# Weights in three loads, one batch's last sums on ScalarE, and a shared last step, in a four-block transformer on one core

## The chip, the cores and the metric

The kernel runs on one core of a Trainium2 chip. A core has five engines that run side by side, each through its own list of instructions in order: TensorE (PE) multiplies matrices and transposes through its array, with weight loads (PEld) that overlap its matmuls; VectorE (DVE), ScalarE (ACT) and GpSimd (POOL) work element by element; SyncE (SP) issues DMAs. An engine waits for another only where an instruction of its list waits on a semaphore. The metric is the device time of one execution in microseconds; the time of a kernel is the median of several executions.

## What is computed

Four blocks, each followed by a sum with its input and a layer norm. Everything is float32, with 8 batches of 512 tokens and 256 channels.

```python
x = L0_attn_x                                        # (8, 512, 256)
x = layernorm(x + retention(x, past_kv, W_qkv, ...)) # 16 heads of 16, decay mask
x = layernorm(x + ffn(x, ternary(W_fc), ternary(W_proj)))   # 1024 wide, gelu, inner norm
x = layernorm(x + linear_attention(x, Wq, Wk, Wv, W1, W2))  # over heads in a token
x = layernorm(x + experts(x, w_router, wi, wo))      # 8 experts, top 2, capacity 160
```

The first block takes q, k and v of a batch from `x @ W_qkv`, forms scores with a decay mask in chunks of 128 tokens, and norms the result over the whole batch. The last block chooses two experts for a token, gathers at most 160 tokens per expert in each of two groups (batches 0 to 3 and 4 to 7), runs `relu(x @ wi) @ wo`, and adds the weighted rows to the tokens. The last line is that sum followed by a layer norm, whose result is the output:

```python
m = mean(x, -1); v = var(x, -1)
return (x - m) / sqrt(v + 1e-5)
```

## The kernel before

The whole kernel is one function, `tile_layers`, that lays the order of the instructions of all engines by hand. Each piece of work is a generator ("stage"): `stage_a0` makes q, k, v of half a batch, `stage_a1` the scores and the first attention of a batch, `stage_a2` its norm, `stage_b` the ffn, `stage_bn` its norm, `stage_c1`, `stage_hd`, `stage_ca` and `stage_c2` the third block, `choose` and `route` the routing, and then the gathers, dispatches and experts of each group, and `finish` the last norm of a batch. `finish_last` does the last rows.

A planner in the kernel runs at build time. `op` (L235) books a stretch on an engine from a time and a cost that are written in the stage, and `flush` emits all booked instructions in the order of their planned starts. This is why most instructions have line L235. `pe(cost)` adds a stage's matmuls to PE's planned time. `either` books the engine that would end first, by the costs given. Booking DVE work as `DVS`, or POOL work as `POOL`, also books a resource named "port", so that in the plan the two do not overlap there. `bank` takes one of the eight PSUM banks, `slot_tile` one of a few buffers of a kind, and `give` and `release` hand them back with a time.

`interleave` decides which stage goes on next on PE: it walks the long string `turns`, one letter for each step of a stream of stages, and takes the first stage of it that can go on. Where PE would wait more than 1.4 us in the plan, it puts in filler matmuls, named `spare` (L405). So a changed cost or a changed string moves instructions on all engines.

The places that the change touches:

- The loads at the start. All plain DMAs go through SP's one list, in order: the identity (L99), x of the first half batch by `fetch_half(0)`, all of W_qkv as one load, the other constants `cst`, `past`, and then, from `prepare_ffn`, four loads of W_fc, four of W_proj, and small ones. The second half batch's x follows when `load_x` asks for it.
- `stage_a0`: four transposes of x into PSUM, a copy to `xT` on ACT or DVE, 4 matmuls for q and 4 for k (L1081), then 4 for v (L1107); a float32 matmul takes two passes through the array, and the profile counts passes, so 16 and 8. q is copied by ACT, scaled by the decay table on POOL (`qd`) and masked on ACT (`qz`, L235); k is scaled on DVE (`kT`); v is copied by ACT (`vz`). The scores (`sc`, L1154) need qz and kT.
- `prepare_ffn` sums |W_fc| and |W_proj| on DVE (`fc_t`, `pr_t`), makes them ternary on DVE and transposes them on PE (`fc_tp`, `pr_tp`).
- The exchange of heads in the third block: `stage_c1` writes q and k to DRAM (`q_d`, `k_d`) and v (`v_d`, eight small stores), `stage_hd` reads them back in another order (`hh`, `vt`), and `stage_ca` multiplies them (`hs`, L1608).
- The combination: `combine` transposes an expert's result (`eo_tp`, L1942), scales it on ACT or DVE (`eo`), and POOL adds its rows to `y_d` in DRAM by an indirect DMA. Each of these waits until the one before it has landed.
- `finish(b)` loads `z`, 512 tokens of `y_d`, by SP and calls `layernorm`. For each of four chunks of 128 tokens, DVE makes the statistics (two instructions, L476 and L477), then a small step with epsilon on DVE, the power -1/2 on POOL, a small step for the offset `nb` on DVE, and four normalisations. For the second group these go to ACT or DVE, whichever would end first (`free`). Batches 6 and 7 wait in the plan until the tokens of the last expert are known.
- The last expert's rows do not go through `y_d`. Its results `eo_0`, `eo_1`, `eo_2` are added to the tokens concerned by matmuls with a 0/1 matrix (`tail_ps`, L2025), after the tokens' other sums were fetched (`tail_y`). `finish_last` adds these, makes statistics and normalises on DVE, and POOL writes the rows over the output by indirect DMAs (L2053), which wait for the plain stores of the output.

## Time and profile before

| | us |
|---|---|
| median of 3 runs | 875.41 (874.04 to 876.87) |
| the profiled run | 876.97 |
| span of its profile, first to last instruction | 874.9 |

| engine | busy us | share |
|---|---|---|
| PE | 822.5 | 94% |
| PEld | 674.0 | 77% |
| DVE | 616.0 | 70% |
| ACT | 513.3 | 59% |
| POOL | 323.4 | 37% |

PE's 822.5 us hold 34.7 us of fillers. The mean granted clock of PE is 0.983 of full speed. In the timeline a line has the start, the duration, the engine, the line of the kernel, the operation, out<-in, the shape and the count; in brackets stand the idle time just before it on its engine and what ended that. In the table by stretches, each engine has its busy time and number of instructions, then follow the granted clock, the mean busy share of the DMA engines, and what they moved. Matmul ends are modelled, so "busy" is not "at peak". A wait for several things is put down to the one that came last.

### The profile page before, as it was taken

To read this page: it belongs to the slowest core of one execution; us is meant where nothing else is said; L and a number is where in the kernel's file an instruction comes from. 1 tells how busy PE (TensorE), PEld (TensorE's weight loads), DVE (VectorE), ACT (ScalarE), POOL (GpSimd) and SP (SyncE) were. 2 spreads that over 40 slices of the span, in tenths; PEclk is the share of its full clock that TensorE was granted. 3 is DMA by queue.
4 is the path that set the end of the run, shared out by engine and by line. 5 is a ranking of instruction groups with operands and counts; after the bars stand their busy time and mean duration, and the time that the engine had idled before them with its cause. 6 is when DMAs were issued, how large, how long until landed. Compare 5 with 4: busy or idle time off the path is not lost. (4 is left out here: it accounts for less than half of the span.)

```text
span 874.9 us, 20462 instructions
## 1 busy us (share of the span) xinstructions
PE 822.5 (94%) x8078; PEld 674.0 (77%) x8078; DVE 616.0 (70%) x1677; ACT 513.3 (59%) x1039; POOL 323.4 (37%) x343
## 2 busy tenths in 40 slices
PE   7999989999999999999899999899999999989982
PEld 5877877876878887787778777677679889779971
DVE  4945687588788788877888898899878444604325
ACT  2435668658764867758788686876745364122221
POOL 1222452344244532343254425415153241362432
PEclk9999999999999999999999999999999999999995
DMA  6153111652722032633523528636577477658352
GB/s 209 31 171 114 44 38 18 116 147 54 180 65 60 23 78 54 165 93 37 151 30 79 161 43 227 200 50 174 147 181 241 139 227 243 179 138 268 78 144 91
DMA packets 201647, 106.89 MB, mean 122 GB/s; under 512 B 124464, under 2 KB 192240, under 8 KB 201360
## 3 DMA queue, kind: packets, MB, share of 16 engines
q1 hardware_dynamic: 197696, 100.01, 42.0%
q0 software_dynamic: 3856, 5.57, 3.5%
q8 instruction: 64, 1.05, 0.5%
q14 instruction: 31, 0.25, 0.1%
HBM read 70.96 MB, written 30.41 MB: 116 GB/s over the span
## 5 line engine op out<-in xcount | busy, mean ns | idle before, releaser
L235 POOL TENSOR_TENSOR fsq<-fsq,fh 128x256 f32<-128x256 f32 x96 | 70.3, 732 | 66.2 <-ACT fh L235 42.5
L235 DVE TENSOR_TENSOR scm<-sc,cst 128x512 f32<-128x512 f32 x109 | 68.7, 681 | 13.0 <-PE sc L1154 12.8
L1384 PE MATMUL fc_ps<-x1T,fcT 128*128 128x256 f32 x512 | 72.1, 291 | 4.4 <-DVE x1T L235 4.4
L235 DVE TENSOR_TENSOR hm<-hs,cst 128x512 f32<-128x512 f32 x111 | 70.4, 681 | 8.2 <-PE hs L1608 8.1
L1384 PEld LDWEIGHTS fc_ps<-x1T,fcT 128*128 128x128 f32 x512 | 64.1, 191 | 8.8 <-DVE x1T L235 4.5
L1425 PE MATMUL pr_ps<-prT,fT 128*128 128x258 f32 x512 | 69.3, 290 | 0.0
L235 DVE SCALAR_TENSOR_TENSOR fT<-fh,lnf,fT 128x256 fp32r<-128x256 f32 x128 | 61.1, 524 | 11.3 <-ACT fT L235 10.8
L1425 PEld LDWEIGHTS pr_ps<-prT,fT 128*128 128x128 f32 x512 | 63.8, 189 | 3.1 <-issue 1.6
L1081 PE MATMUL qk_ps<-xT,wqkv 128*128 128x256 f32 x256 | 62.4, 396 | 3.2 <-DMA wqkv<-in_L_attn_W_qkv 1.9
L235 POOL DMA_INDIRECT y_d<-eo,srci x21 | 32.7, 1557 | 82.7 <-issue 22.9
L1900 PE MATMUL wo_ps<-e_hT,wo 128*128 128x160 f32 x416 | 63.2, 305 | 0.0
L1516 PE MATMUL qk_ps<-x2T,l1T 128*128 128x512 f32 x128 | 59.6, 600 | 1.0 <-ACT x2T L235 1.0
L1900 PEld LDWEIGHTS wo_ps<-e_hT,wo 128*128 128x128 f32 x416 | 58.9, 193 | 1.6 <-issue 0.9
L1872 PE MATMUL wi_ps<-xsT,wi 128*128 128x160 f32 x416 | 60.0, 300 | 0.0
L1081 PEld LDWEIGHTS qk_ps<-xT,wqkv 128*128 128x128 f32 x256 | 49.2, 198 | 13.0 <-issue 3.3
L235 ACT ACTIVATE fT<-fh,lnf 128x256 fp32r<-128x256 f32 x128 | 58.2, 499 | 1.5
L1872 PEld LDWEIGHTS wi_ps<-xsT,wi 128*128 128x128 f32 x416 | 57.4, 190 | 0.8 <-ACT xsT L235 0.5
L235 POOL TENSOR_TENSOR ln<-ln,mhalf 128x4 f32<-128x4 f32 x32 | 33.7, 1054 | 56.1 <-DVE ln L235 54.1
L235 ACT ACTIVATE e_hT<-wi_ps 128x480 f32<-128x480 f32 (+1 forms) x48 | 24.8, 523 | 47.0 <-PE wi_ps L1872 45.3
L235 POOL TENSOR_TENSOR scm<-scm,cst 128x512 f32<-128x512 f32 x19 | 24.3, 1281 | 59.8 <-ACT scm L235 22.4
L235 ACT ACTIVATE fh<-fh 128x512 f32<-128x512 f32 x64 | 39.5, 626 | 9.4 <-DVE fT L235 8.4
L1608 PE MATMUL hs<-hh 16*128 16x128 f32 x1024 | 41.1, 292 | 4.1 <-DMA hh<-q_d 2.7
(286 smaller groups left out, 1945.0 us busy)
## 6 DMA issues: line engine op xcount, KB each, us to landing
wi<-in_L_ffn_wi SPq DMA_DIRECT2D x10, 1024.0 KB
wo<-in_L_ffn_wo SPq DMA_DIRECT2D x10, 1024.0 KB
hh<-k_d SPq DMA_DIRECT2D x32, 256.0 KB
hh<-q_d SPq DMA_DIRECT2D x32, 256.0 KB
xh<-in_L_attn_x SPq DMA_DIRECT2D x16, 256.0 KB
x<-in_L_attn_x SPq DMA_DIRECT2D x8, 512.0 KB
k_d<-qk SPq DMA_DIRECT2D x32, 128.0 KB
q_d<-qk SPq DMA_DIRECT2D x16, 256.0 KB
```

Of the source, the lines that this page charges most:

```text
L235: heapq.heappush(Plan.events, (t, Plan.count, shares, t + cost, lambda: fn(*args, **kw)))
L1081: T.matmul(ps[:, m * HT : (m + 1) * HT], wqkv[:, k, which * D + m * P : which * D + (m + 1) * P], xT[:, k, :], start=(k == 0), stop=(k == ...
L1384: T.matmul(ps[:, j * HT : (j + 1) * HT], fcT[:, k, f * P : (f + 1) * P], x[:, k, :], start=(k == 0 and x is low), stop=(k == NK - 1 and x ...
L1425: T.matmul(acc[:, : D + 2], hs[:, part, f, c * P : (c + 1) * P], prT[:, f, :], start=(f == 0 and part == 1), stop=(f == NF - 1 and part == 0),
L1516: T.matmul(ps, l1T[:, k, which, m * P : (m + 1) * P], x2T[:, k, :], start=(k == 0), stop=(k == NK - 1),)
L1608: T.matmul(sc[r][:, g * P : (g + 1) * P], hh[rows, a * D + z : (a + 1) * D : 2], qh[rows, :, 16 * a + z : 16 * a + 16 : 2], start=True, st ...
L1872: T.matmul(ps[:, f * CAP : (f + 1) * CAP], wi[k][:, (f3 + f) * P : (f3 + f + 1) * P], x[:, k, es], start=(k == 0), stop=(k == NK - 1),)
L1900: T.matmul(ps[:, m * CAP : (m + 1) * CAP], parts[2 + f // 4][:, f % 4, m * P : (m + 1) * P], hT[:, f, :], start=(f == 0), stop=(f == NF - 1),)
```

## The change

- W_qkv is loaded in three parts (q, k and v columns), and x of the second half batch right behind them, ahead of the constants.
- `layernorm` gets a form `summed`, used for batch 5: ACT makes the sums of each chunk (a copy with an accumulated output, L235), DVE the mean and its negative (`centres`), ACT the sums of squares about the mean, DVE the variance.
- The second choice for the normalisations of batches 4 to 7 is POOL at 0.56 instead of DVE at 0.42.
- Some 20 planned costs are set to other values, among them the landing of a scatter into `y_d` (2.5 to 3.0) and the start of the last stores.
- The string `turns` is another one.

```diff
-    def layernorm(pool, dst, src, ts, on_act=False, keep=False, free=False):
+    def layernorm(pool, dst, src, ts, on_act=False, keep=False, free=False, summed=False):
...
+        def centres():
+            nc.vector.tensor_scalar(nb, sums[:, 0, :], -1.0 / D, None, ALU.mult)
+            return nc.vector.tensor_scalar(mv[:, :, 0], sums[:, 0, :], 1.0 / D, None, ALU.mult)
...
-        for c in range(NC):
+        if summed:
+            waste = slot_tile(pool, "ex", [P, D], "waste")
+            sums = ln[:, : 2 * NC].rearrange("p (i c) -> p i c", i=2)
+            for c in range(NC):
+                t = op(
+                    ACT, 0.43, max(ts[c], Plan.slot_of[id(ln)][3]), A.activation, waste, src[:, c, :], AF.Copy,
+                    accum_out=sums[:, 0, c : c + 1], use=waste,
+                )
+            t = op(DVS, 0.14, t, centres, use=ln)
+            for c in range(NC):
+                t = op(
+                    ACT, 0.43, t, A.activation, waste, src[:, c, :], AF.Square,
+                    bias=nb[:, c : c + 1], accum_out=sums[:, 1, c : c + 1], use=waste,
+                )
+            give(waste, t)
+            t = op(DVS, 0.08, t, V.tensor_scalar, mv[:, :, 1], sums[:, 1, :], 1.0 / D, None, ALU.mult)
+        for c in range(0 if summed else NC):
             t = op(DVE, 0.61, ts[c], stats, c, use=ln)
...
-                        DVS, 0.42, V.tensor_scalar,
+                        POOL, 0.56, GP.tensor_scalar,
...
-        dma(0.0, wqkv, ins["L0_attn_W_qkv"].rearrange("(k p) n -> p k n", p=P))
+        w_in = ins["L0_attn_W_qkv"].rearrange("(k p) n -> p k n", p=P)
+        for cols in (slice(D), slice(D, 2 * D), slice(2 * D, 3 * D)):
+            dma(0.0, wqkv[:, :, cols], w_in[:, :, cols])
+        fetch_half(1)
...
-            t = Plan.t + (4.0 if i == 0 else 22.0 if i < 4 else 5.0)
-            if i > 0:
+            t = Plan.t + (4.0 if i == 0 else 8.0 if i == 1 else 14.0 if i < 4 else 5.0)
+            if i > 1:
...
-            t = pe(0.36)
+            t = pe(0.3)
...
-                Plan.landed = done + 2.5
+                Plan.landed = done + 3.0
...
-                t = op(POOLD, 1.2, max(t, tail["stored"]), put, j, n)
+                t = op(POOLD, 1.28, max(t, tail["stored"] + 1.2), put, j, n)
...
-            e = max(layernorm(wk, z, z, [landing] * NC, on_act=(g == 1), free=(g == 1)))
+            e = max(layernorm(wk, z, z, [landing] * NC, on_act=(g == 1), free=(g == 1), summed=(b == B - 3)))
...
-            "cbhnbbnbbcblbbnlellnlbeeerblnbeeeeeeleebelllbbbleebcllclllbcleebbbelbeeneblllenrnnnl"
...
+            "nbblbhbcbnbblebllleeccbbnelebeeeeeleeeblnllbbbleelblclllnbcleebbbeelbeenllelnbnnnlnc"
...
```

The order of the built program of each kernel can be listed. In the new one, batch 5's eight sums stand on ACT between the second group's first normalisations and the scaling of `eo_0`; `eo_1` stands behind batch 5's two normalisations on ACT; and two of the four normalisations of each of the batches 4 to 7 stand on POOL. PE has 4845 matmuls instead of 4846, of which 70 instead of 71 are fillers, and three of them stand in the tail.

More of the change, by code (lines that the diff above doesn't have):

```diff
@@ L1161, in scores @@
                         T.transpose(ps[:, m * P : (m + 1) * P], kT[:, m, cs], ident)
-                t = pe(1.35 if c < NC - 1 else 1.0)
+                t = pe(1.32 if c < NC - 1 else 1.04)
                 give(qz[c], t)
@@ L1226, in stage_a1 @@
                             )
-                t = pe(1.95 if c < NC - 1 else 1.55)
+                t = pe(1.97 if c < NC - 1 else 1.58)
                 for sm in scm:
@@ L1293, in stage_a2 @@
             t = op(
-                DVE, 0.15, pe(0.2), V.tensor_scalar, gs[:, 0:1], ps[:, 0:1], -1.0 / P, None, ALU.mult,
+                DVE, 0.15, pe(0.15), V.tensor_scalar, gs[:, 0:1], ps[:, 0:1], -1.0 / P, None, ALU.mult,
                 bank=ps,
@@ L1300, in stage_a2 @@
             T.matmul(ps[:, 0:1], ones, gs[:, 1:2], start=True, stop=True)
-            t = rsqrt(gs[:, 2:3], ps[:, 0:1], 1.0 / P, LN_EPS, pe(0.2), bank=ps)
+            t = rsqrt(gs[:, 2:3], ps[:, 0:1], 1.0 / P, LN_EPS, pe(0.15), bank=ps)
             ga = wk.tile([P, 2, 2], F32, tag="gn_a", name=f"gn_a_{b}")
@@ L1315, in stage_a2 @@
                 e1 = op(
-                    ACT, 0.47, t, A.activation, r[:, 0, :], r[:, 0, :], AF.Identity,
+                    ACT, 0.59, t, A.activation, r[:, 0, :], r[:, 0, :], AF.Identity,
                     bias=ga[:, 1, 0:1], scale=ga[:, 0, 0:1],
@@ L1319, in stage_a2 @@
                 e2 = op(
-                    POOL, 0.5, t, GP.tensor_scalar, r[:, 1, :], r[:, 1, :], ga[:, 0, 1:2],
+                    POOL, 0.56, t, GP.tensor_scalar, r[:, 1, :], r[:, 1, :], ga[:, 0, 1:2],
                     ga[:, 1, 1:2], ALU.mult, ALU.add,
@@ L1367, in stage_b @@
                 pv = ps.rearrange("p (k t) -> p k t", k=NK)
-                t = pe(0.5)
+                t = pe(0.47)
                 based = op(
@@ L1391, in stage_b @@
                     inner_ = op(
-                        GELU, 0.6, pe(0.97), A.activation, hv, ps, AF.Gelu, use=h, bank=ps
+                        GELU, 0.58, pe(0.95), A.activation, hv, ps, AF.Gelu, use=h, bank=ps
                     )
@@ L1440, in stage_b @@
                     t = op(
-                        DVE, 0.19, pe(2.35 if c == 1 else 1.95), V.tensor_reduce, nmu,
+                        DVE, 0.19, pe(2.32 if c == 1 else 1.98), V.tensor_reduce, nmu,
                         acc[:, D : D + 2], AX.X, ALU.add,
@@ L1556, in stage_c1 @@
                 t = op(
-                    ACT, 0.65, pe(1.73), A.copy, v[:, 2 * half : 2 * half + 2],
+                    ACT, 0.58, pe(1.72), A.copy, v[:, 2 * half : 2 * half + 2],
                     ps.rearrange("p (g h d) -> p g h d", g=2, d=HD), bank=ps,
@@ L1679, in stage_c2 @@
                 e = op(
-                    ACT, 0.5, e, A.activation, sq, a[:, c, :], AF.Square, accum_out=rs[:, c : c + 1],
+                    ACT, 0.42, e, A.activation, sq, a[:, c, :], AF.Square, accum_out=rs[:, c : c + 1],
                     use=sq, drop=sq if c == NC - 1 else None,
@@ L1851, in dispatch @@
                 done = copied(
-                    pe(0.57), (0.43, 0.5), xsT[g, pair][:, k, :], ps[:, : 2 * CAP], bank=ps
+                    pe(0.52), (0.43, 0.5), xsT[g, pair][:, k, :], ps[:, : 2 * CAP], bank=ps
                 )
@@ L1878, in expert_in @@
                 e = op(
-                    ACT, 0.57 if n == 3 else 0.44, pe(0.55 * n), A.activation, dst,
+                    ACT, 0.57 if n == 3 else 0.44, pe(0.544 * n), A.activation, dst,
                     ps[:, : n * CAP], AF.Relu, bank=ps,
@@ L1904, in expert_out @@
                     if f % 4 == 3 and (m, f) != (NK - 1, NF - 1):
-                        pe(1.09)
+                        pe(1.087)
                         yield from need(0.0, n=0)
-            t = pe(1.09)
+            t = pe(1.087)
             done = copied(
@@ L1947, in combine @@
                 t = either(
-                    pe(0.24), (ACT, 0.47, A.activation, (eo[:n], ps[:n, :D], AF.Copy), {"scale": gate}),
+                    pe(0.22), (ACT, 0.47, A.activation, (eo[:n], ps[:n, :D], AF.Copy), {"scale": gate}),
                     (DVE, 0.42, V.tensor_scalar, (eo[:n], ps[:n, :D], gate, None, ALU.mult), {}),
@@ L2123, in tile_layers @@
         streams = {
-            "x": [(("x", i), after(("x", i - 1)), {"xh": 1} if i else {}, load_x(i)) for i in range(2 * B)],
+            "x": [(("x", i), after(("x", i - 1)), {"xh": 1} if i > 1 else {}, load_x(i)) for i in range(2 * B)],
             "a0": [
@@ L2210, in tile_layers @@
         turns = (
-            "cbhnbbnbbcblbbnlellnlbeeerblnbeeeeeeleebelllbbbleebcllclllbcleebbbelbeeneblllenrnnnl"
-            "cnnblcnnbbbnclncbnncbrllbblllnnnhlbchlnhjhhlhnnblbbcbnclnhnhcnbbcnnbbblnjlllnbbnjllj"
-            "bbjbnjjbjbbchljjnhnlhjhhhjlhlbnjhhnllnblcffnfnjjncfllljnnfjjlclnbbjclnbbjlnlbjlcjbbn"
-            "jbnllbnjlncjffchnbnlnfflhblcbnhnnlnllnncnznllhbflbbnnnljfflbbhfflhbblbhlhhlfffflllll"
-            "fcnlnnlnbcjbjnfjffhfjbjnnnbnbhljcffjnjhjnnnhjbhjbhfnncnjncfhjhhlbblfblhllhnnhfnnlqfq"
-            "hjfhnhnjnncffhcjjjcnnlnfhcfjcjljnfhlfjlnnnnffjjfnjffnnnljjhjhhhhhhhfffhjjnnnnfcfcnjc"
-            "fjnnffnccfnnnnfjfhfnjnnjjnffjjjhhhhjjnnnmmnhfhmhojfjjhfjffnnnjnffjffnjnjffjofohfjohf"
-            "hojohohhohjohjjohjfffjffffffrjjfffjfrrmmfrjrjrmjrqqmqrqjmmpmmjqjfffqffjjfqfffqrqqjqj"
-            "rfffqqfpfrrqpqrpprqrqqrrqpfmpfqfffqffqrffrqrrqqpffffrrfrpqqrpqqpqqoprrrrpqorppoooooo"
-            "ooqqqrrrrrrppqmqqpmmmqppppmmqmmmqrqrqrrqrqqrqrrprpqpqrrqqqqrrppqqqqqqqqprpqpqrrqqqqm"
-            "rqqmqqqqppqqpmppqqrrrqrprprrrpzpzzypz"
+            "nbblbhbcbnbblebllleeccbbnelebeeeeeleeeblnllbbbleelblclllnbcleebbbeelbeenllelnbnnnlnc"
+            "nblcnbnbcnrblnccbbllbrnnblcllnnbhjnlhblnhhhhnblnblbnlncchnbchcbnnbnblrbnjjllblnclblj"
+            "jbbbnjnjjbbbbbhljjhnnhljhlhhhljnhjhnllcnlfffnjncjflnllnnjjlcjlfcbnbjnlbbbjllnbbjlnjb"
+            "jnclnlbbljhcnnjnbffnffhlhllnnnnlcjjllnnzbncnclhllbbbfnnlfbflbhfflbbbhllnhhlhffffllnl"
+            "llfhlnnflcnnjcffbbfjnbnnjbbfnclhfjhnjnjbjjnbnhhjhjnjfnnfcchhqjhlbfbbnllhllhmhmmnnnnf"
+            "fljfhjhhnqfncfjnnhcjjcjnnlffnchjcljfnhlfjnnfnjnjffjfnnflnnjlhjhhhhhhhfjjffhjnnnnfcfc"
+            "jncfjnnncfcffnnnnfjffjnnhnjjnjfjfjhhhhjnjnnpnhhohjjjfffhjffnnnnjfffjfnjnfojffjjhfooh"
+            "fhoohorhhjjohhojjohjfffjffffffjjffmfjrrfmfjrjrqmqqjrrjjmjqqrfmmmmmffqffjjfjfpfqfqrqq"
+            "qjqrffqfqffprqrrqpprrqqrqrffpfrqqffqffffrqprrqpfqfffrfprrqrpqppqoqrqrqrrqmrorppopooo"
+            "ooooprrmrpqqqqqprrmpqpprpmqqmmrqqrqrqrqmrrqqqqqpprqrqmpqqmppqrrrrqqprppqrmqqqqqrrqpq"
+            "qpmrqqmpqpqqqqqrqrprrqrrprqpqzzzzyppp"
         )
```

## The prediction

> **What bounds the kernel now.** I read the busy time of the engines in stretches of 25 us first, because the order of all engines is laid by hand-made planning and a mean over the span hides its ends.
>
> ```profile
> core 0: us, PE busy (x) PEld busy (x) DVE busy (x) ACT busy (x) POOL busy (x), PEclk, DMA share, GB/s
> 0.00:25.00 25.00, 18.74 (x137) 14.59 (x138) 12.06 (x32) 7.23 (x14) 4.14 (x8) 1.00 0.65 193
> 250.00:275.00 25.00, 25.00 (x344) 20.53 (x346) 21.61 (x55) 12.85 (x26) 8.70 (x11) 1.00 0.24 69
> 425.00:450.00 25.00, 22.34 (x248) 17.52 (x247) 20.75 (x54) 20.41 (x46) 9.50 (x11) 0.93 0.33 99
> 850.00:875.00 25.00, 5.93 (x16) 3.73 (x16) 13.10 (x50) 4.97 (x10) 7.43 (x11) 0.62 0.31 103
> ```
>
> TensorE (PE) is full nearly everywhere: 822.5 us of 874.9. Of the 52.4 us that it is not busy, 6.3 lie in the first 25 us and 19.1 in the last 25. So there are three places to win: the start, the end, and the waits between. The start, from the timeline:
>
> ```profile
> 4.09 1.09 PE L1054 MATMUL tp<-cst_ident,xh 128*128 128x128 f32 x4 [4.09 <-DMA xh<-in_L_attn_x]
> 5.21 0.58 ACT L235 COPY xT<-tp 128x512 f32<-128x512 f32 x1 [3.21 <-PE tp L1054]
> 7.10 6.52 PE L1081 MATMUL qk_ps<-xT,wqkv 128*128 128x256 f32 x16 [1.93 <-DMA wqkv<-in_L_attn_W_qkv]
> 13.46 1.89 PE L1107 MATMUL v_ps<-wqkv,xT 128*128 128x256 f32 x8
> 15.45 0.58 ACT L235 COPY vz<-v_ps 128x512 f32<-128x512 f32 x1 [3.97 <-PE v_ps L1107]
> 16.89 1.15 PE L1154 MATMUL sc<-qz,kT 32*128 32x256 f32 x16 [0.24 <-ACT qz L235]
> ```
>
> PE has x transposed at 5.79 and then waits for all of wqkv until 7.10. The q and k matmuls run at 6.36/16 = 0.40 us each, the v matmuls at 0.236: the array is slow until about 13 us. The first scores wait for qz, which stands behind vz on ScalarE (ACT), which waits for the v matmuls. So PE sets the start. The end:
>
> ```profile
> 841.81 2.02 SPq L235 DMA_DIRECT2D z<-y_d  x4
> 843.42 4.51 PE L1900 MATMUL wo_ps<-e_hT,wo 128*128 128x160 f32 x32
> 845.85 0.43 DVE L476 BATCH_NORM_STATS2 ln<-z 128x6 f32<-128x256 f32 x1 [6.10 <-DMA z<-y_d]
> 853.76 0.48 DVE L235 COPY eoT<-wo_ps 128x320 f32<-128x320 f32 x1
> 855.56 4.81 PE L2025 MATMUL tail_ps<-eo,tail_same 128*128 128x256 f32 x12
> 859.92 1.07 DVE L235 TENSOR_TENSOR tail_y<-tail_y,tail_ps 128x256 f32<-128x256 f32 x3
> 862.07 0.42 DVE L2045 BATCH_NORM_STATS2 tail_st<-tail_y 128x6 f32<-128x256 f32 x1
> 866.31 1.05 POOL L2053 DMA_INDIRECT out<-tail_y,tail_row  x1 [0.64 <-DVE tail_y L235]
> ```
>
> PE's last expert product is done at 847.9, but its copy eoT stands on VectorE (DVE) behind the statistics of batches 4 and 5 and runs at 853.76. DVE is the bound from 845.9 to 864.4. From the first tail statistics (862.07) to the end are 12.8 us. The waits between, and the price of a sum on ACT:
>
> ```profile
> 432.18 1.73 PE L1608 MATMUL hs<-hh 16*128 16x128 f32 x32 [2.66 <-DMA hh<-q_d]
> 838.82 0.41 PE L1942 MATMUL eo_tp<-cst_ident,eoT 128*64 128x128 f32 x2 [0.57 <-ACT eoT L235]
> L405 PE MATMUL spare<-cst,cst_ident 128*128 128x256 f32 x142 | 34.7, 386 | 0.0
> 705.25 0.42 ACT L235 ACTIVATE rms_sq<-a 128x256 f32<-128x256 f32 x1 [0.47 <-DVE a L235]
> 705.79 0.42 ACT L235 ACTIVATE rms_sq<-a 128x256 f32<-128x256 f32 x1
> ```
>
> **Part 1, the start.** wqkv lands 3.0 us after xh (4.09 to 7.10), so its first third lands some 1.0 us after it, at 5.1, before xT is there (5.79). PE then starts q at about 5.9: 1.2 us earlier. The second and third thirds (6.1, 7.1) are in time, since q takes 8 x 0.40 = 3.2 us. SyncE (SP) issues three more DMAs (two of wqkv, xh of half 1) ahead of the constants: 3 x 0.45 = 1.4 us of issue, and 256 KB more on the wire. The four W_fc loads of that size follow one another, in stretches that move about 350 GB/s, so that is 0.75 us more for everything behind: past, on which DVE starts at 9.00, the constants and W_fc. DVE then does state preparation (2.3 us) and two reductions (1.3) before kT: ready at 9.75+2.3+1.3+0.7 = 14.1 instead of 14.35, still before the scores. So the later data is hidden; were it 1 us later still, kT would set the scores. Clock: PE ran slow from 7.10 to about 12.8, 5.7 us. If it stays slow as long, the v matmuls end at 14.0 instead of 15.2: 1.2 gained. If it turns at 9.4 (one step of the clock record, 3.41 us, earlier), q, k and v end at 13.0: 2.2 gained. If it stays slow for two such steps, 6.8 us, 0.8. The ten fillers ("spare") and all matmuls up to the first transposes of W_proj are the same in both orders, and DVE, which is full from 18 to 37 us, has the same work; so the gain is kept. I take 1.6 (0.8 to 2.3).
>
> The four W_fc loads of 256 KB stand behind one another on the same queue, and from 9 to 13 us, while they and W_proj land, the DMA engines move 351 to 383 GB/s: a load of this size costs its bytes and no more. Against the split speaks the Trainium skill (DMA: Bandwidth & Descriptors, "Anatomy of one DMA" and "Measured"): some 2 us are fixed in each transfer, and loads should be batched to 1 MiB. If these added up, an estimate by that page would put two more loads at 4 us, kT at 18.1, the scores 1.3 later than before, and the whole sum at -1.1 instead of -4.0.
>
> **Part 2, the middle.** The string of turns is replaced and some costs are retuned. The order of instructions as built shows the same matmuls (only spare: 71 to 70 in all, 57 instead of 61 between the start and the tail), moved by a few places. Four fillers fewer at 34.7/71 = 0.49 us are 2.0 us, if the waits that they stood for are gone, and nothing if the waits stay. The eo_tp that waited 0.57 us at 838.8 now stands behind the next wi matmuls: 0.57 gained. Against it: in the third batch the first hs matmul of the head exchange (q written to DRAM and read back, as at 432 us) stands 17.7 us of PE work behind its q matmuls instead of 20.2, while the fourth batch at 18.2 waited 2.66 us; but three instead of five v_d stores (about 1 us each) now lie between the last q_d store and the hh loads on SP. I price that at half a wait, +1.3. Sum 0 - 2.0 - 0.6 + 1.3, about -1.0. The bounds are the whole waits: PE's gaps of over 0.4 us between 59 and 839 us sum to 22 us in 24 places. A new order can close a fifth of them or open as many: -4 to +4.
>
> **Part 3, the end.** Scatters into y_d run as a chain, each behind the landing of the last, some 4.6 us apart, and z loads wait for its end (841.81). In the new order two of the producing transposes stand earlier on PE, one later; by their matmul counts the fifth-last scatter can start at 817.8 rather than 818.69. So z comes 0.9 us earlier against PE's end. Batch 5's statistics leave DVE (4 x 0.53 = 2.1 us) and become 8 sums on ACT at 0.54 (705.25 to 705.79) = 4.3 us; eight normalisations leave DVE (8 x 0.37 = 2.9 us) for GpSimd (POOL) at 0.56 (the row of q<-q,gn_a), 1.1 per batch beside ACT's 1.09, so nothing on the path. Walk, on before's clock: z4 at 844.8, z5 at 846.3; ACT's four plain sums to 848.6; DVE centres to 849.0, eoT at 849.8 instead of 854.2. But the two eo scalings now both stand on ACT: behind z4's two steps (850.4) and four squares (852.7) comes eo_0 at 853.2, behind z5's two steps (855.6) eo_1 at 856.0, as late as before (855.9). DVE itself stands in order behind the squares until 852.8, then does batches 6 and 7 (8 x 0.53), six small ones and two waits for POOL's power (1.02 each) to 859.6; PE's last ten passes at 0.40 end at 860.1. Three adds: tail statistics from 860.7 instead of 862.07. Gain 1.4. Were z not earlier: 0.7 or, with POOL at its slowest row (1.04), a loss of 0.7; were it 2 us earlier: 2.7. So most of what DVE gains is given to ACT.
>
> **Sum**: -1.6 - 1.0 - 1.4 = -4.0 on the span of 874.9, that is 870.9. The profiled run took 877.0, 1.6 more than the median; against the median of 875.4 it gives **871.4**.
>
> **Rivals.**
> - *The middle gives it back.* For it: the waits sit where DVE and ACT are late, and both have the same work. Against: fewer fillers. With one new exchange wait of 2.66 beside the two ends: -3.0 + 2.7 = -0.3: 875.1. No change.
> - *The exchange opens gaps.* At hs<-hh (L1608) a wait of 2.66 us was followed by a 3.41 us stretch at half clock (the 0.93 of 425:450), 1.7 us more: 4.4 each. One costs more than the ends gain; from the second on the kernel is slower by over 0.3%: -3.0 + 8.8 = +5.8: 881. For it: one such wait already there and the third batch now as close. Against: fewer stores ahead of the reads.
> - *The split does nothing* (thirds run beside each other on the 16 engines and land together): start 0, the rest -2.4: 873.0.
>
> **Numbers.** Forecast 0.50, middle gives back 0.24, exchange 0.13, split idle 0.13. A measurement tells about 0.3%, 2.6 us, from no change. Faster: most of the forecast case (its own range is 868 to 873.5) and half of the split's: 0.60. Same 0.27; slower 0.13. Range: the bounds of the parts added as independent, -7.5 to +1.5: 867.5 to 877.
>
> **What would show it.** Start: the q matmuls at 5.9 and sc at 14.7 to 15.7. End: eoT within 2 us of the last wo matmul, DVE idle until ACT's squares are done, eo_1 some 8 us after the last wo, tail statistics about 12.8 us after it instead of 14.2. Middle: PE's waits over 0.4 us summing to about 20 us, with no half-clock stretch added. Wrong would be: kT later than the v matmuls, eo_1 the last thing for 3 us more, or a wait of 2 us and more at L1608's new line in the third batch.

## The result: slower by half a per cent, and the profile after

The changed kernel takes 878.54 us (median of 20 runs, 874.88 to 884.57) against 875.0 for the kernel before beside it (20 runs, 871.64 to 881.52): a ratio of 1.0048 (95% interval 1.0026 to 1.0070), some 4 us slower where 4 us faster were forecast. A second measurement, in a later session, gave 1.0036 (1.0017 to 1.0056). The profiled run took 877.75 us with a span of 876.0.

By stretches of the span (columns as before), the changed kernel has this:

```profile
core 0: us, PE busy (x) PEld busy (x) DVE busy (x) ACT busy (x) POOL busy (x), PEclk, DMA share, GB/s
175.00:200.00 25.00, 23.70 (x302) 19.67 (x301) 18.96 (x51) 12.83 (x27) 11.07 (x13) 0.93 0.53 151
425.00:450.00 25.00, 22.98 (x288) 18.66 (x286) 21.74 (x58) 20.58 (x47) 8.19 (x8) 0.93 0.46 123
550.00:575.00 25.00, 24.50 (x272) 19.15 (x272) 21.59 (x59) 20.94 (x41) 10.22 (x12) 0.94 0.52 170
575.00:600.00 25.00, 24.60 (x215) 17.80 (x214) 23.00 (x63) 16.34 (x35) 7.39 (x6) 0.93 0.43 61
```

PE is busy for 828.5 us instead of 822.5, though it has one matmul less: it is busier because it is slower. The granted clock, the third column from the right, is below 1.00 in 175:200, 550:575 and 575:600, and not only in 425:450. In the same table of the kernel before it is 1.00 in these three:

```profile
175.00:200.00 25.00, 23.82 (x364) 19.68 (x362) 20.74 (x55) 13.33 (x28) 13.28 (x15) 1.00 0.55 159
550.00:575.00 25.00, 22.36 (x270) 17.50 (x270) 21.55 (x55) 20.38 (x44) 8.42 (x10) 1.00 0.54 171
575.00:600.00 25.00, 24.57 (x228) 18.50 (x228) 22.74 (x62) 18.88 (x38) 8.57 (x8) 1.00 0.49 82
```

In the clock record of the trace each such dip is one step of 3.41 us at half speed. Between the first scores and the last wo there are six of them, at 61, 184, 437, 550, 594 and 761 us; before had three, at 61, 433 and 757. A step costs half its length, 1.7 us.

The waits of PE between 17 and 845 us did not grow (columns: what waited, for whom, us in total, times, longest):

```profile
PE hs L1631 <- DMA hh<-q_d: 3.3, 2, 2.0
...
PE tp L1386 <- ACT x L235: 1.3, 1, 1.3
```

The longest, at the exchange, is 2.0 us where it was 2.7. All waits of over 0.4 us between 17 and 845 us come to 17.1 us, before to 22.0. The start of the changed kernel, from the timeline:

```profile
6.08 5.75 PE L1104 MATMUL qk_ps<-xT,wqkv 128*128 128x256 f32 x16 [0.68 <-ACT xT L235]
11.67 1.89 PE L1130 MATMUL v_ps<-wqkv,xT 128*128 128x256 f32 x8
...
15.10 1.15 PE L1177 MATMUL sc<-qz,kT 32*128 32x256 f32 x16 [1.10 <-ACT qz L235]
...
10.18 0.35 DVE L775 SCALAR_TENSOR_TENSOR state<-cst,past 64x64 f32<-64x64 f32 x2 [9.33 <-DMA past<-in_L_attn_past_kv]
...
12.62 1.27 POOL L235 TENSOR_TENSOR qd<-q,cst 128x512 f32<-128x512 f32 x1 [10.49 <-DVE state L780]
```

q starts at 6.08 and the scores at 15.10 instead of 16.89, so this profile is 1.8 us ahead of that of before. But past is used at 10.18 instead of 9.00, and POOL's qd, which waits for DVE's last state step, runs at 12.62 instead of 11.56. The end:

```profile
843.53 2.02 SPq L235 DMA_DIRECT2D z<-y_d  x4
...
844.87 4.51 PE L1923 MATMUL wo_ps<-e_hT,wo 128*128 128x160 f32 x32
...
847.58 0.43 DVE L480 BATCH_NORM_STATS2 ln<-z 128x6 f32<-128x256 f32 x1 [15.45 <-DMA z<-y_d]
...
851.54 0.48 DVE L235 COPY eoT<-wo_ps 128x320 f32<-128x320 f32 x1
...
852.85 10.79 SPq L2131 DMA_DIRECT2D out<-z  x4
...
854.54 0.51 ACT L235 ACTIVATE waste<-z,ln 128x256 f32<-128x256 f32 x1
...
855.17 0.38 DVE L235 TENSOR_SCALAR ln<-ln 128x4 f32<-128x4 f32 x2 [3.15 <-ACT waste L235]
...
857.87 0.45 ACT L235 ACTIVATE eo<-eo_tp,sgate 128x256 f32<-128x256 f32 x1
...
858.38 4.83 PE L2048 MATMUL tail_ps<-eo,tail_same 128*128 128x256 f32 x10 [2.12 <-ACT eo L235]
...
863.58 0.41 DVE L2068 BATCH_NORM_STATS2 tail_st<-tail_y 128x6 f32<-128x256 f32 x1
...
867.37 1.07 POOL L2076 DMA_INDIRECT out<-tail_y,tail_row  x1 [0.19 <-issue]
```

The last wo ends at 849.38 (844.87 + 4.51), 1.45 us later than before, so 3.2 us went between the first scores and here. eoT is copied 2.2 us behind it, but DVE then idles 3.15 us for ACT's squares, eo_1 (857.87) stands behind them and behind batch 5's normalisations, and the tail's statistics come 14.2 us after the last wo, as before (14.1). From the first use of z to the end are 28.4 us (876.0 - 847.6); before it was 29.0 (874.9 - 845.9). The four plain stores of the output (`out<-z`) are issued until 863.64 (852.85 + 10.79), and the first write of the last rows starts at 867.37; the part on the tail comes back to these two.

### The profile page after: what moved, and what is told of

The parts are those of the page before. It is cut to its first block, busy times and chain, and to the rows that moved or that the text cites. A ratio compares the mean times of both kernels' runs of the same rounds, so it can differ in the third digit from the quotient of the medians.

```text
span 876.0 us, 20470 instructions
## 1 busy us (share of the span) xinstructions
PE 828.5 (95%) x8076; PEld 676.6 (77%) x8076; DVE 610.7 (70%) x1661; ACT 517.5 (59%) x1058; POOL 329.3 (38%) x351
## 5 line engine op out<-in xcount | busy, mean ns | idle before, releaser
L235 POOL TENSOR_TENSOR fsq<-fsq,fh 128x256 f32<-128x256 f32 x96 | 70.9, 739 | 60.7 <-ACT fh L235 38.3
L235 DVE TENSOR_TENSOR scm<-sc,cst 128x512 f32<-128x512 f32 x110 | 69.4, 680 | 13.2 <-PE sc L1177 13.1
L235 DVE TENSOR_TENSOR hm<-hs,cst 128x512 f32<-128x512 f32 x110 | 70.1, 680 | 9.1 <-PE hs L1631 8.8
L1448 PE MATMUL pr_ps<-prT,fT 128*128 128x258 f32 x512 | 71.4, 293 | 1.1 <-DVE fT L235 1.1
L235 DVE SCALAR_TENSOR_TENSOR fT<-fh,lnf,fT 128x256 fp32r<-128x256 f32 x128 | 61.3, 525 | 12.3 <-ACT fT L235 12.0
L235 POOL DMA_INDIRECT y_d<-eo,srci x21 | 34.0, 1618 | 73.5 <-issue 25.7
L235 ACT ACTIVATE fT<-fh,lnf 128x256 fp32r<-128x256 f32 x128 | 58.0, 499 | 1.4
L235 POOL TENSOR_TENSOR ln<-ln,mhalf 128x4 f32<-128x4 f32 x32 | 33.2, 1037 | 60.3 <-DVE ln L235 57.8
L235 ACT ACTIVATE e_hT<-wi_ps 128x480 f32<-128x480 f32 (+1 forms) x48 | 24.7, 524 | 51.7 <-PE wi_ps L1895 51.0
L235 ACT ACTIVATE fh<-fh 128x512 f32<-128x512 f32 x64 | 39.5, 627 | 12.2 <-DVE fT L235 11.3
L235 POOL TENSOR_TENSOR scm<-scm,cst 128x512 f32<-128x512 f32 x18 | 23.1, 1283 | 57.1 <-ACT scm L235 24.3
```

The lines of the kernel that those rows point to most:

```text
L235: heapq.heappush(Plan.events, (t, Plan.count, shares, t + cost, lambda: fn(*args, **kw)))
L1448: T.matmul(acc[:, : D + 2], hs[:, part, f, c * P : (c + 1) * P], prT[:, f, :], start=(f == 0 and part == 1), stop=(f == NF - 1 and part == 0),
```

## The experiments

All ratios are to the kernel before, run beside each on the same chip, with 95% intervals. "Clock" is the mean over a kernel's runs of the clock granted over the span; one half-clock step lowers it by 3.41/2/875 = 0.0019. The kernel before has 0.982 to 0.984 in the five sessions in which these were measured.

| kernel | ratio | interval | clock |
|---|---|---|---|
| again (before, unchanged) | 0.9997 | 0.9980 to 1.0013 | 0.983 |
| start_only | 1.0015 | 0.9994 to 1.0035 | 0.981 |
| split_only | 0.9987 | 0.9964 to 1.0011 | 0.981 |
| cst_first | 1.0001 | 0.9983 to 1.0019 | 0.982 |
| tail_only | 1.0002 | 0.9984 to 1.0020 | 0.984 |
| start_order (after without the tail part) | 1.0033 | 1.0011 to 1.0056 | 0.980 |
| turns_only | 1.0027 | 1.0004 to 1.0050 | 0.979 |
| costs_only | 1.0041 | 1.0024 to 1.0058 | 0.981 |
| after_again (after, unchanged) | 1.0036 | 1.0017 to 1.0056 | 0.980 |
| after_real | 1.0037 | 1.0014 to 1.0059 | 0.979 |
| before_fill | 1.0052 | 1.0032 to 1.0071 | 0.988 |
| after_fill | 1.0063 | 1.0043 to 1.0083 | 0.989 |
| before_fill_mid | 1.0010 | 0.9988 to 1.0031 | 0.987 |
| after_fill_mid | 0.9989 | 0.9971 to 1.0008 | 0.988 |
| fill_part | 1.0036 | 1.0017 to 1.0055 | 0.982 |
| fill_big (7 runs) | 1.0064 | 1.0039 to 1.0088 | 0.986 |
| fill_real | 1.0002 | 0.9987 to 1.0017 | 0.988 |
| fill_cst | 0.9998 | 0.9983 to 1.0012 | 0.988 |

### Which part costs it

Four kernels ran together: the kernel before again, two with one part of the change alone, and the changed kernel without its tail part.

start_only, against before:

```diff
-        dma(0.0, wqkv, ins["L0_attn_W_qkv"].rearrange("(k p) n -> p k n", p=P))
+        for cols in (slice(D), slice(D, 2 * D), slice(2 * D, 3 * D)):
+            dma(0.0, wqkv[:, :, cols], w_in[:, :, cols])
+        fetch_half(1)
```

tail_only, against before (with the new `layernorm`; start_order is the changed kernel with these lines and `layernorm` as before):

```diff
-                Plan.landed = done + 2.5
+                Plan.landed = done + 3.0
-                t = op(POOLD, 1.2, max(t, tail["stored"]), put, j, n)
+                t = op(POOLD, 1.28, max(t, tail["stored"] + 1.2), put, j, n)
-            e = max(layernorm(wk, z, z, [landing] * NC, on_act=(g == 1), free=(g == 1)))
+            e = max(layernorm(wk, z, z, [landing] * NC, on_act=(g == 1), free=(g == 1), summed=(b == B - 3)))
```

The orders on the engines of start_only are those of before, and of tail_only up to the tail.

> The kernel before, unchanged, for the granted clock of each of its runs, which is known so far for one run only (0.983). Theory A (the new order of the middle leaves PE waiting inside more of the 3.41 us steps of the clock record, and each half-clock step costs 1.7 us): the mean clock of these runs is 0.981 to 0.984, above the 0.9785 mean of the changed kernel's twenty runs, and the longer runs are those with the lower clock. Rival B (the tail costs the time) and rival C (plain waits of PE in the middle): the clocks are about the same as the changed kernel's.

> The kernel before with only the three loads of W_qkv and x of half batch 1 behind them; the order on PE, DVE, ACT and POOL is that of before. Theory A: -1.2 to -2.0 us, as in the changed kernel's profile, where the first scores start at 15.10 instead of 16.89. Rival C: the gain is eaten by DVE behind it, within 0.5 us of before.

> The kernel before with only batch 5's sums on ACT, POOL as second choice of the last normalisations, and the two tail costs; the order before the tail is that of before. Theory A: -0.5 to +0.5 us, since in the changed kernel's profile the tail's statistics start 14.2 us after PE's last wo, and 14.1 before. Rival B: slower by 2 us or more.

> The changed kernel without its tail part (layernorm, landing and store costs as before); its order until the tail is the changed kernel's. Theory A: +3 to +5 us against before, as the changed kernel, with a mean clock of about 0.979. Rival B: faster than before by 1 us or more. Rival C: +3 to +5 with PE's waits in the middle longer than before's 25 us and a clock as before's.

The tail part costs nothing (1.0002), and the changed kernel without it is about as slow as with it (1.0033, 2.9 us). So rival B falls. The clock is 0.983 and 0.984 in again and tail_only and 0.980 with the new order. But start_only, which has the order of before, has 0.981 too. Against the kernel before beside them, the early loads alone go with a clock that is 0.0021 lower (start_only) and 0.0014 lower (split_only, below), each known to some 0.002, and the kernels with the new order with one that is 0.003 to 0.004 lower. So part of the clock's loss, perhaps half, goes with the early loads. What the order adds is plainer in the time: +1.3 and -1.1 us for start_only and split_only, +2.4 to +4.2 us for the five measurements with the new order. Among the twenty runs of the changed kernel the clock goes from 0.988 to 0.973 and the time from 874.9 to 884.6, 0.82 us for each 0.001, or 1.6 us for each half-clock step.

start_only missed: 1.2 to 2.0 us faster was expected, and its interval reaches only to 0.5 us faster. The profile of the unchanged kernel's second run tells one reason:

```profile
6.56 5.07 PE L1081 MATMUL qk_ps<-xT,wqkv 128*128 128x256 f32 x16 [1.23 <-DMA wqkv<-in_L_attn_W_qkv]
...
14.90 1.15 PE L1154 MATMUL sc<-qz,kT 32*128 32x256 f32 x16 [0.24 <-ACT qz L235]
```

This is the timeline of PE. Here q starts at 6.56 and the scores at 14.90, with no change at all. Over four profiles of kernels that load W_qkv in one piece (before_fill, where a filler stands ahead of q, left out) the scores start at 14.90, 15.89, 16.04 and 16.89 (W_qkv lands between 6.2 and 7.1, and the clock turns to full speed between 9.4 and 12.8 us). The profile that the prediction was made from was the latest of them.

The timeline of tail_only also shows what the new sums can do on ACT when the order differs:

```profile
846.59 0.42 ACT L235 ACTIVATE waste<-z 128x256 f32<-128x256 f32 x1 [3.94 <-DVE ln L480]
...
847.00 0.42 ACT L235 ACTIVATE e_hT<-wi_ps 128x320 f32<-128x320 f32 x1
...
847.47 4.66 PE L1920 MATMUL wo_ps<-e_hT,wo 128*128 128x160 f32 x20 [2.72 <-ACT e_hT L235]
```

There the first sum stands ahead of the last e_hT and waits for z, and the last wo waits 2.72 us for e_hT. The changed kernel has e_hT first, and no such wait.

### The string or the costs

turns_only is the kernel before with the early loads and the new string; costs_only has the early loads, the retuned costs, and the old string; both have the tail of before. In lines, against start_order (of turns_only's costs, some 16, one is shown):

```diff
 turns_only
-            t = pe(0.3)
+            t = pe(0.36)
...
 costs_only
-            "nbblbhbcbnbblebllleeccbbnelebeeeeeleeeblnllbbbleelblclllnbcleebbbeelbeenllelnbnnnlnc"
+            "cbhnbbnbbcblbbnlellnlbeeerblnbeeeeeeleebelllbbbleebcllclllbcleebbbelbeeneblllenrnnnl"
...
```

> The kernel before with the early loads and the new string of turns, all planned costs and the tail as before; the order on PE differs from that of the changed kernel in 9 places, from that of before in 178. Theory A (the string's order costs the time, through more half-clock steps and 2 us of slower matmuls): mean clock 0.979 to 0.980, 2.5 to 4.5 us slower than before. Rival (the retuned costs do it): within 1.5 us of before, clock 0.982 to 0.983.

> The kernel before with the early loads and the retuned costs, the old string of turns and the old tail; the order on PE differs from that of before in 21 places. Theory A: within 1.5 us of before, clock 0.981 to 0.983. Rival: 2.5 us or more slower, clock 0.979 to 0.980.

turns_only is as expected of the string: clock 0.979, 1.0027. costs_only missed (1.0041), and its profile says why it tells little: the old string with the new due time of half batch 1 puts that half's q and k ahead of the first scores (timeline).

```profile
16.51 3.15 PE L1084 MATMUL qk_ps<-xT,wqkv 128*128 128x256 f32 x8 [2.51 <-ACT xT L235]
19.59 1.62 PE L1157 MATMUL sc<-qz,kT 32*128 32x256 f32 x16
```

The scores start at 19.59, some 4 us late, where the loss by time is 3.6; behind them it has four half-clock steps, as kernels with the old order have. So the string makes the new order and its clock, and the costs by themselves were not tried apart from the early loads.

From the traces, PE's time from the first scores to the end of the last wo can be taken apart. "Half" is half of PE's busy time inside half-clock steps, fillers count 0.489 each, and the rest is all other matmul time at full clock (gaps of up to 0.15 us, about 1 us in all, are left out):

| profiles | from scores to wo | waits over 0.15 | half-clock steps | lost to half | fillers | rest |
|---|---|---|---|---|---|---|
| old order, mean of 6 | 832.4 | 25.6 | 4.3 (2 to 7) | 7.3 | 33.3 | 765.6 |
| new order, mean of 5 | 837.7 | 24.5 | 7.2 (6 to 8) | 12.1 | 33.0 | 766.8 |
| after_fill_mid | 833.1 | 10.4 | 1 | 1.7 | 61.1 | 759.1 |
| before_fill_mid | 835.6 | 11.8 | 3 | 5.1 | 62.1 | 756.4 |

(Old: before, again, start_only, split_only, cst_first, tail_only. New: after, after_again, start_order, after_real, turns_only.) Of the 5.3 us between the first two rows, 4.8 are half-clock steps and 1.2 slower matmuls; the waits are 1.1 shorter. So rival C falls as well. The steps by profile, in the order of the lists, are 3, 4, 4, 7, 2, 6 and 6, 8, 6, 8, 8: they overlap, and split_only has seven with the order of before. Three of the 36 of the second row stand between 17 and 24 us (two in after_again, one in turns_only) and go with the early loads (see The start); they are 1.0 of the 4.8 us. Two places tell the orders apart: a step between 181 and 191 us is in four of the five profiles with the new order and in one of the six with the old, and one between 594 and 600 us in three of the five and in none of the six. The step behind the exchange, between 431 and 447 us, is in all eleven.

With more fillers the rest shrinks too, by 8 to 9 us, though the other matmuls are the same. That is not explained here, so of the 4.6 us by which the stretch is shorter in after_fill_mid than with the new order no share can be put on the clock alone.

### Fillers in more waits

Where PE's matmuls are thin the clock should fall, and fillers should hold it. after_fill and before_fill change the bounds in `interleave`; the _mid kernels do so only behind 20 us of the plan:

```diff
-            if on_pe and t - Plan.now > 1.4 and Plan.now > 0.0 and min(Plan.banks) <= Plan.now:
+            if on_pe and t - Plan.now > (1.4 if t < 20.0 else 0.9) and Plan.now > 0.0 and min(Plan.banks) <= Plan.now:
-                while t - Plan.now > 0.9:
+                while t - Plan.now > (0.9 if t < 20.0 else 0.45):
```

> The changed kernel with fillers wherever the plan shows PE waiting over 0.9 us (1.4 before), down to 0.45: 133 fillers instead of 70, all other engines' order the same. Clock theory (waits that leave a 3.41 us step of the clock record short of array work are followed by a half-clock step of 1.7 us): mean clock of the runs 0.981 or more instead of 0.979, and 1 to 4 us faster than the changed kernel. Rival (plain waits and slower matmuls, not the clock): the clock rises or not, and the time stays or grows by up to 10 us, as 63 fillers of 0.49 us run in part where the plan is wrong.

> The kernel before with the same rule for fillers: 135 instead of 71. Clock theory: mean clock above 0.984 (0.983 without), faster by 0 to 3 us. Rival: slower, by up to 10 us.

> The changed kernel with the lower bounds for fillers (0.9 and 0.45 us) only behind 20 us of the plan, so that no filler stands ahead of q and waits for the constants (which put the first scores at 21.4 instead of 15.1 with the bounds lowered everywhere). Clock theory: clock 0.988 or more, and the 6.3 us of the start come back: 4 to 6 us faster than with the bounds lowered everywhere, that is within 1.5 us of the kernel before and 3 us or more faster than the changed kernel. Rival (half-clock steps are a symptom, the fillers cost what they save): no faster than the changed kernel, +4 against before.

> The kernel before with the same rule behind 20 us. Clock theory: the old order has two half-clock steps less to win (0.983 against 0.979), so the fillers bring 0 to 2 us at most, against 3 and more in the changed kernel. Rival: as slow as with the bounds lowered everywhere, +3 to +5.

In the first two the clock is as the theory had it (0.988 and 0.989) and the time as its rival. One place of the timeline of after_fill tells most of that:

```profile
10.68 2.08 PE L405 MATMUL spare<-cst,cst_ident 128*128 128x256 f32 x4 [5.44 <-DMA cst<-in_constants]
12.55 5.62 PE L1104 MATMUL qk_ps<-xT,wqkv 128*128 128x256 f32 x16
```

A filler ahead of q reads the constants, which land at 10.7, and the scores start at 21.4. Without it the changed kernel comes back to the time of before: after_fill_mid 0.9989 against 1.0036 to 1.0048, with a clock of 0.988. In its profile by stretches the dips of the middle are gone:

```profile
175.00:200.00 25.00, 23.60 (x309) 19.87 (x308) 20.39 (x54) 13.11 (x28) 12.22 (x14) 1.00 0.51 152
425.00:450.00 25.00, 24.11 (x293) 18.13 (x292) 22.72 (x60) 20.97 (x49) 8.42 (x10) 1.00 0.48 125
550.00:575.00 25.00, 24.25 (x303) 19.45 (x296) 21.95 (x56) 20.82 (x43) 8.69 (x11) 1.00 0.53 169
575.00:600.00 25.00, 25.00 (x235) 19.29 (x234) 23.21 (x62) 18.40 (x37) 7.83 (x7) 1.00 0.46 67
```

The kernel before gains nothing by the same rule (1.0010), as expected: it has fewer half-clock steps to win and pays as much for the fillers. That the new order's loss can be won back by array work in its waits is shown. That the clock is all of it is not, as the next runs say.

> The changed kernel itself, beside the kernels with more fillers. All theories: +2 to +6 us against before, mean clock 0.978 to 0.980.

> The changed kernel with 92 fillers instead of 70: behind 20 us each planned wait of over 0.9 us is filled down to 0.9. Clock theory in its strict form (the clock is the whole loss, and what keeps it is array work in the waits): clock 0.981 to 0.984, between the changed kernel's 0.979 and the 0.988 of 129 fillers, and the time lies between theirs, 1 to 3 us faster than the changed kernel. Rival (the gain came from something else in the 129, such as waits hidden by the extra matmuls): same clock, no gain.

> The changed kernel with 103 fillers: only planned waits of over 1.1 us, filled down to 0.45. Clock theory: long waits are those that leave a step short of work, so the clock is nearly that of 129 fillers, 0.985 to 0.988, and with 26 fewer fillers the time is 0 to 3 us below it: before's time or up to 3 us faster. Rival: clock 0.982 or less, no faster than 129 fillers.

fill_part has 0.9 for both bounds, fill_big 1.1 and 0.45. fill_part raised the clock from 0.980 to 0.982, as the theory had it, and gained nothing (1.0036, like after_again beside it), as its rival had it: its 22 added fillers are 10.8 us of matmuls, which by the times cost what they save. fill_big has a clock of 0.986 and was slower still (1.0064, over only seven runs, 873.8 to 881.7), though its profile has one half-clock step and a span of 872.0 (that run is the fastest of the seven; the clock of the others is 0.981 to 0.988). That contradicts the strict form of the theory, and I can't explain it.

### The tail

after_real plans batch 5's sums at what they take:

```diff
-                    ACT, 0.43, max(ts[c], Plan.slot_of[id(ln)][3]), A.activation, waste, src[:, c, :], AF.Copy,
+                    ACT, 0.55, max(ts[c], Plan.slot_of[id(ln)][3]), A.activation, waste, src[:, c, :], AF.Copy,
-                    ACT, 0.43, t, A.activation, waste, src[:, c, :], AF.Square,
+                    ACT, 0.66, t, A.activation, waste, src[:, c, :], AF.Square,
```

> The changed kernel with batch 5's sums planned at what they take on ACT (0.55 and 0.66 instead of 0.43): by the order both eo scalings then stand ahead of batch 5's normalisations on ACT, and two of batch 6's four statistics ahead of the wait for the squares on DVE; all before the tail stays. Tail theory (the tail gives away its gain because eo_1 waits behind ACT's squares and DVE idles behind them): from the landing of z to the end 26.5 to 27.5 us instead of 28.4, the kernel 1 to 2 us faster than the changed one, +2 to +3 against before. Rival (the chain through POOL's powers binds whatever stands where): 28 us or more from z to the end, no gain.

> 129 fillers, less those of the tail, and batch 5's sums planned at what they take. Tail theory: from z to the tail statistics 14.9 to 15.4 instead of 16.0, but the last stores of the output bind the end: 0 to 0.7 us faster than 129 fillers alone, which were 0.1% faster than before. Rival (the tail gain counts in full): 1 us or more.

The end of after_real, from its timeline:

```profile
851.12 0.43 DVE L480 BATCH_NORM_STATS2 ln<-z 128x6 f32<-128x256 f32 x1 [12.54 <-DMA z<-y_d]
...
858.60 0.82 ACT L235 ACTIVATE eo<-eo_tp,sgate 128x256 f32<-128x256 f32 x2
...
866.07 0.42 DVE L2068 BATCH_NORM_STATS2 tail_st<-tail_y 128x6 f32<-128x256 f32 x1
...
871.21 1.07 POOL L2076 DMA_INDIRECT out<-tail_y,tail_row  x1 [1.53 <-DVE tail_y L235]
```

In after_real both eo follow the squares at once, and the tail's statistics come 14.95 us after z (866.07 - 851.12) instead of 16.0. Not all of that is eo_1's place: in the changed kernel's second profile, with the same order, they come 15.4 us after z. There the last ten passes of `tail_ps` took 3.58 us; in the first they ran at half clock and took 4.83. So eo_1's place was worth some 0.4 us.

But POOL's first write of the last rows then waits 1.53 us (0.19 in the changed kernel's first profile). By the code it also waits for the plain stores of the output, and the profiles bear that out. Here are these stores in before (its write starts at 866.31) and in after_real, from the timelines:

```profile
850.82 12.09 SPq L2108 DMA_DIRECT2D out<-z  x4
...
856.41 11.34 SPq L2131 DMA_DIRECT2D out<-z  x4
```

The last of them is issued at 862.91 and at 867.75, and the write starts 3.4 and 3.5 us later. That distance is 3.4 to 3.5 us in 18 of the twenty profiles, however early the rows are ready. In the other two, after and fill_part, it is 3.7: there the last ten passes of `tail_ps` took 4.83 us, and the rows themselves came last. So the plain stores bind the end, and the tail's statistics add at most 0.3 us. The last store is issued 17.1 us after z in before, 16.1 in the changed kernel and 16.6 in after_real, each time 0.4 us behind the end of the last normalisation, which stands on ACT in before and on POOL in the other two.

From z to the end it is 28.7 us in after_real, as in the other profiles with the new tail (28.1 to 28.7; 28.7 to 29.3 with the old one). The tail theory was right on the statistics and wrong on the end, and its rival had the outcome; that POOL's powers are what holds the last normalisation was not tried. fill_real came no faster than after_fill_mid (1.0002).

### The start

split_only leaves x of half batch 1 where it was; cst_first loads the q columns, then the constants and past, then the k and v columns; fill_cst does that in fill_real:

```diff
 cst_first
-        dma(0.0, wqkv, ins["L0_attn_W_qkv"].rearrange("(k p) n -> p k n", p=P))
+        dma(0.0, wqkv[:, :, :D], w_in[:, :, :D])
         dma(0.0, cst, ins["constants"][:, P:n_const])
...
+        for cols in (slice(D, 2 * D), slice(2 * D, 3 * D)):
+            dma(0.0, wqkv[:, :, cols], w_in[:, :, cols])
```

> The kernel before with W_qkv in three loads, and x of half batch 1 where it was. Start theory (q starts earlier but the first scores wait for kT, which DVE makes late because past and the constants land later behind the added loads): past is used at 9.3 to 9.8 us instead of 8.5 to 9.0 (10.0 to 10.6 with x ahead of it), the first scores at 14.3 to 15.0; 0 to 1 us faster than before. Rival (the earlier q is worth its 1.2 us or more): 1.2 to 2 us faster.

> The kernel before with the q columns of W_qkv first, then the constants and past, then the k and v columns; x of half batch 1 where it was, the order on all engines that of before. Start theory (with three loads the scores wait for past: DVE's state steps stand ahead of POOL's qd and DVE's kT): past is used at 8.5 or earlier instead of 10.3 (three loads) and 8.5 to 9.0 (before), q starts at 5.8 to 6.0, qd at 11 or earlier, the scores 1.5 to 1.6 us behind the end of v; k must not wait for its columns. 0 to 1.5 us faster than before. Rival (PE now waits for the k columns): a wait of 0.5 us or more inside the sixteen q and k matmuls, no gain.

> 129 fillers but those of the tail, the sums planned at what they take, and the constants and past ahead of the k and v columns with x of half batch 1 behind all: the version that should beat both if the start's gain adds to it. Start theory: past at 8.5 or earlier, scores at 14.5 to 15.0, no half-clock step at 17; 0.5 to 1.5 us faster than without (which was at before's time), so 0 to 1.5 us faster than before. Rival: the same as without, within 0.5 us of before.

In split_only past is used at 10.26, within the range with x ahead of it (9.97 to 11.35 in twelve profiles): most of the delay comes from the two added loads, not from the bytes of x. Its scores came at 15.05 and its time at 0.9987: no gain that can be measured. In cst_first past is used at 9.29, not by 8.5, the scores at 15.89, and nothing is gained; in fill_cst at 8.42 and 15.21, and nothing either. In both the scores stand 1.54 us behind the end of v, as in before and in the changed kernel's first profile: there the slow q, k and v matmuls bind. With past late it is 1.8 to 2.4 us in four profiles (start_only, after_again, after_real, turns_only), where the clock is full by 9.0 to 11.0 us and qd is what comes last. What the early loads can lose shows in the timeline of the changed kernel's second profile:

```profile
13.31 1.27 POOL L235 TENSOR_TENSOR qd<-q,cst 128x512 f32<-128x512 f32 x1 [11.18 <-DVE state L780]
...
15.57 1.15 PE L1177 MATMUL sc<-qz,kT 32*128 32x256 f32 x16 [1.73 <-ACT qz L235]
...
16.93 1.71 PE L817 MATMUL fc_ps<-fc_t,cst 128*128 128x1 f32 x8
18.50 3.76 PE L1104 MATMUL qk_ps<-xT,wqkv 128*128 128x256 f32 x8
```

Past is used at 10.87, qd at 13.31, and PE waits 1.73 us for the scores. The clock, full since 10.1 us, falls back to half at 16.9 for two steps, and eight q and k matmuls take 3.76 us instead of 1.97. Five of the fifteen profiles with the early loads have such a step at 17 us (after_again, turns_only, costs_only, fill_real, fill_cst), none of the five without them.

## Why the prediction was wrong

**The start, -1.6 (0.8 to 2.3).** The steps were right as far as they can be seen in one profile: q at 5.9 (6.08), the scores at 14.7 to 15.7 (15.10). The term was mis-sized, because it was set against a single profile whose W_qkv and clock were late. Against the mean of four (15.93), the eleven profiles with three loads of W_qkv, constants behind them, average 15.4 (costs_only and after_fill left out), so 0.5; and some of them pay 1.7 us or more for a clock that falls back. By time it is +1.3 us (-0.5 to +3.1) in start_only. The "0.75 us more for everything behind" was 1.3 to 2.7 us (past at 9.97 to 11.35 in the twelve profiles with x ahead, without the early loads 8.7 in the mean of five). Nor did the 4 us come that the prediction worked out from the Trainium skill (DMA: Bandwidth & Descriptors, "Anatomy of one DMA"); that page gives its 2 us for transfers issued through GpSimd, and these are issued by SP. The check "kT at 14.1, still before the scores" missed POOL's qd, which waits for DVE's state steps and holds the scores in four profiles.

**The middle, -1.0 (-4 to +4).** This step failed: up to z it came to +4.7 instead. "Four fillers fewer are 2.0 us, if the waits that they stood for are gone" counted waits, and the waits did shrink: those of over 0.4 us come to 17 us instead of 22 in the first two profiles ("about 20" was forecast), and to 19.5 instead of 22.2 in the means of the table's two groups. What was not counted is the clock: half-clock steps were priced only at the exchange, and "no half-clock stretch added" was listed as what would be seen. The kernels with the new order have three more in the mean of the profiles (7.2 instead of 4.3), 4.8 us, of which 1.0 belongs to the early loads, and 1.2 us of slower matmuls. Putting 59 more fillers in brought the time back, 22 more did not; whether the four that the order gave up would have held the clock is not shown.

**The end, -1.4 (-2.7 to +0.7).** In these two profiles z was not 0.9 us earlier: it is 1.8 us ahead of the last wo's end, before 2.1, and the chain of scatters, from the one at about 800 us to the last, took 37.8 us in both. Over more profiles that is open: z is 1.8 to 4.8 us ahead in five with the order and tail of before (2.2 in the middle one) and 1.8 to 4.7 in the five with the new order (4.5). The walk held up to eo_1 (eoT 2.2 us after wo, eo_1 at 8.5 us, DVE idle behind the squares), though the four squares came 0.63 us apart (852.65 to 854.54) and not 0.54; the last ten passes of `tail_ps` took 4.83 us instead of 4.0. But its last step had the wrong path: it counts 12.8 us to the end from the tail's statistics, while the end hangs on the last plain store, in before as well. What was won behind z, 0.6 us (29.0 to 28.4), goes with that store, issued 1.0 us earlier after z. That the bound given for "z not earlier", 0.7, is near it is luck. By time the tail part alone is +0.2 us (-1.4 to +1.7) in tail_only.

**The sum.** -0.5 for the start, +4.7 between the first scores and z (829.0 and 833.7 us in the means of the table's two groups), -0.6 behind z, gives +3.6, beside a measured 0.48% and 0.36% (4.2 and 3.1 us). The rival "the exchange opens gaps" had the right mechanism, half-clock stretches from the order, and the wrong place: the longest wait at hs<-hh is 2.0 us instead of 2.7 here, 2.2 to 2.7 in the other four profiles with the new order, and the step behind it is in both orders. "The split does nothing" was nearly right on its own term. The range was too narrow since each bound came from one profile: the unchanged kernel alone has 3 and 4 steps in its two profiles, and a clock of 0.975 to 0.988 over its runs. (The lower bound, 867.5, does not quite follow: 875.4 - 7.5 is 867.9. And 5.79 is the end of ACT's copy xT; PE's transposes end at 5.18. Nothing hangs on either.)

## What to carry to other kernels

Where TensorE is full, count its half-clock steps, not only its waits, and over several runs: their phase differs from run to run, so that one profile's three steps may be another's seven. Before pricing an earlier transfer, look at more than one start of the unchanged kernel, and follow every engine behind the transfers that are pushed back, not only the one that ends last in the profile. A filler has to read data that is there, and its own time has to be won back: here 59 of them, 0.49 us each, won the loss back, and 22 won nothing. At the end, look for what the last write waits for before pricing the path to its data.

## What the runs showed of the hardware

The half-clock steps lie on a grid of 3.41 us whose phase differs from run to run: within each profile they start a multiple of 3.41 us apart, but at 60.6, 60.2, 59.5 or 61.6 us for the same wait. Over six profiles (before, after, again, start_only, tail_only, start_order), of the grid steps at full clock between 20 and 848 us, all in which PE waited 1.8 us or more were followed by one at half clock, between 1.1 and 1.8 us some were and some not, and below that none was, but for two with only 0.4 us of waits, of this kind (from the timeline of the changed kernel, where the step from 590.5 to 593.9 is followed by one at half clock):

```profile
590.81 0.88 PE L1631 MATMUL hs<-hh 16*128 16x128 f32 x6
592.08 1.22 PE L1631 MATMUL hs<-hh 16*128 16x128 f32 x26 [0.40 <-ACT x2n L235]
```

These matmuls use 16 of the 128 rows. Weighted by the rows and columns of the array that they use and by the columns that stream through it, and counted where a matmul starts, the work of a grid step parts the two kinds better than the waits do: of the 1,421 steps, the 27 that a half-clock step followed are among the 71 with the least work (by the waits alone, among the 143 with the longest). This is a reading of six profiles, and no run varied the rows alone.

The Trainium skill (TensorE: Matmul & The Clock Gate, "HAM oscillation") gives as its rule that gaps of over about 3.4 us matter. No wait in the middle was longer than 2.7 us in these profiles, and by that rule none of the changed kernel's six steps would be there. The same page ("What's actually happening") says that the window of 3.41 us runs freely, and the traces agree.
